# Order of the six projections of a tile, place of the norms behind them, and the means of the first norm in a fused attention and feed-forward kernel

## The chip, the cores and the metric

The kernel runs on one core of a Trainium2 chip. The metric is the time of one execution on the device, in microseconds (us); the time before is the median of three runs. The profile is that of one execution. Engines are called PE (TensorE, matmuls), PEld (its weight loads), DVE (VectorE), ACT (ScalarE), POOL (GpSimd) and SP (the engine that issues the DMAs).

## What is computed

The input x has 16 sequences of 256 positions with 128 channels. It goes through a first attention (windows of 64, 16 heads of 8 channels, a layer norm ahead of it and one on queries and keys), and then through a second block: a layer norm and six layers, each of a local attention and a gated feed-forward part. Cut to what matters here:

```python
x = x + first_attention(layernorm(x))
y = layernorm(x)
for i in range(6):
    # local attention: 16 heads of 64, windows of 32 that see the one before
    q, k, v = split(shift_tokens(y) @ Wqkv[i])        # 128 -> 3 x 1024
    q, k = l2norm(q) * q_scale[i], l2norm(k) * k_scale[i]
    q, k = rotary(q), rotary(k)
    y = softmax(mask(8 * q @ k.T)) @ v @ Wo[i] + y
    # feed-forward: layer norm, two products, gelu
    a, gate = split(layernorm(shift_tokens(y)) @ W1[i] + b1[i])
    y = (a * gelu(gate)) @ W2[i] + b2[i] + y
return x + y
```

## The kernel before

**Two stages.** The first attention works on 8 units of 4 tiles of 128 positions, its steps for several units merged into one order. Its `row_stats` (lines 315 to 328) makes mean and spread of each row: for the norm ahead of the attention (`pre == "a"`) ACT takes four copies with accumulation (line 321), for the one behind it DVE takes one sum (line 323) and POOL scales it (line 324). It takes about the first 250 us of the span.

The main stage, six layers, goes over 192 tiles of 128 positions (32 a layer) as a pipeline: in the turn of tile t, PE does the projections of tile t (`stage_p`), the scores of tile t-1 (`stage_s`), the exponentials of t-2 (`stage_e`), the weighted sums of t-3 (`stage_v`), the output product of t-5 (`stage_w`), and a part of the feed-forward of earlier tiles (`stage_f`, which serves four tiles at once and is spread over four turns).

**The order of the work.** Each stage is a generator; `merge_at` (line 248) steps them in the order of places between 0 and 1 in a turn. `stage_p` is stepped at 0, 1/6, ... 5/6 (`AT_P`), the exponentials at 0.09 and 0.095, the weighted sums at 0.1 and 0.45, the output product at 0.47, the scores at 0.72. The feed-forward goes by `AT_F = ((0.86,), (0.06, 0.74, 0.88), (0.03, 0.27, 0.8), (0.1, 0.35, 0.6))`, one tuple for each of four turns: its steps are the centring (0.86), the spread with a logarithm and an exponential (0.06 of the second turn), three gelus (0.74, 0.88, and 0.03 of the third turn), three products with the other half (0.27, 0.8, 0.1), the last matmul (0.35) and the end. PE's instructions keep exactly this recorded order, since `pin` (line 253) chains every matmul (`mul`, line 290) and transpose (`flip`, line 293) to the one before. The other engines' instructions are ordered by the framework's scheduler within their dependencies.

**Two extra orders on ACT.** Gelu and the pair logarithm and exponential are in different activation tables, and a load stands where the table changes. The program keeps them apart by hand: `tab` (line 274) records a logarithm or exponential behind the last gelu recorded; `gelu` (line 280) records the first gelu of a group behind all `tab` instructions recorded since the last first gelu, and the others only behind the gelu before. Behind the third gelu the program puts a load of the table that holds both logarithm and exponential (line 892).

```python
def tab(*args, **how):
    made = S.activation(*args, **how)
    if opened:
        behind(made, opened[-1])
    before.append(made.ins)
```

**A tile's projections.** `project` (line 626) makes three matmuls of 512 columns into one of two banks used in turn (kind "p"), with four of the waiting transposes (`turn`: the keys, queries and probabilities of earlier tiles) hung on them. The kernel before goes through keys, keys, queries, queries, values, values (`for s in (1, 0)`, line 648: s is 1 for keys, 0 for queries; two halves of 8 heads each). Behind a key or query projection, DVE multiplies with the rotary table (line 656), ACT squares into `sq` (line 664), POOL adds the two rotary halves (line 667); behind a value projection ACT copies into `vb` (line 677), one of three buffers used in turn.

`norm` (line 639) closes a pair of halves: DVE sums the squares (line 640), ACT takes logarithm and exponential through `tab` (lines 641 and 642, recorded at line 275), POOL bounds the result and multiplies both halves (lines 643 and 646). The list `late` delays it: the norm of the keys is recorded with the first query projection (third place), that of the queries with the first value projection (fifth place). After the sixth projection SP issues the DMAs that copy `vb` into shifted buffers (lines 688 to 694), read by `stage_v` three tiles later.

The banks of kind "t", "w", "f" and of the first half of `stage_v` are four in one ring (`SPLIT`, `USE`, `USE_V`): transposes, the output product, the feed-forward and the first half of the weighted sums take them one after the other.

Of the kernel before, what the change touches and what calls it, by code (L numbers as in the profile page):

```python
# [14 lines left out]
AF = mybir.ActivationFunctionType  # L15
ALU = mybir.AluOpType
AX = mybir.AxisListType
# [5 lines left out]
NV = 3  # L23
# [32 lines left out]
def kernel(  # L56
# [23 lines left out]
    V, S, G, T = nc.vector, nc.scalar, nc.gpsimd, nc.tensor  # L80
# [193 lines left out]
# [5 lines that stand above are left out]
# [11 lines left out]
    def mul(*args, **how):  # L290
        pin(T.matmul(*args, **how))  # L291
# [5 lines left out]
    def first_attention(p1, p2, p3, pqp, psp0, pop, pyp, ptp=None):  # L297
        ptp = ptp or pyp
        def rsqrt(dst, src, scale):
            if dst.shape[1] != 128:  # L300
                S.activation(dst, src, AF.Ln, bias=epst, scale=scale)
                S.activation(dst, dst, AF.Exp, scale=-0.5)
                return
            n = dst.shape[1]
            a = p3.tile([128, n], F32, name=f"rqa{n}")
            b = p3.tile([128, n], F32, name=f"rqb{n}")
            V.tensor_scalar(b, src, scale, EPS, ALU.mult, ALU.add)
            S.activation(a, b, AF.Ln)
            S.activation(a, a, AF.Exp, scale=-0.5)
            V.tensor_tensor(b, b, a, ALU.mult)  # L310
            V.tensor_tensor(b, b, a, ALU.mult)
            V.tensor_scalar(b, b, -0.5, 1.5, ALU.mult, ALU.add)
            V.tensor_tensor(dst, b, a, ALU.mult)

        def row_stats(xt, pre):
            mu = p3.tile([128, 4], F32, name=f"{pre}mu")
            rs = p3.tile([128, 4], F32, name=f"{pre}rs")
            sq = p3.tile([128, 128], F32, name="sq0")
            if pre == "a":
                for t in range(4):  # L320
                    S.activation(sq, xt[:, t], AF.Copy, scale=-1.0 / 128.0, accum_out=mu[:, t : t + 1])
            else:
                V.tensor_reduce(mu, xt, AX.X, ALU.add)
                G.tensor_scalar(mu, mu, -1.0 / 128.0, None, ALU.mult)
            for t in range(4):
                S.activation(sq, xt[:, t], AF.Square, bias=mu[:, t : t + 1], accum_out=rs[:, t : t + 1])
            rsqrt(rs, rs, 1.0 / 128.0)
            return mu, rs
# [39 lines left out]
        def stage_load(u):  # L368
            if u:
                load_x(u)  # L370
            e = U[u]
            _, e.rs = row_stats(e.xt, "a")
            e.rv = p1.tile([128, 4], F32, name="rv")
            G.tensor_scalar(e.rv, e.rs, VPRE, None, ALU.mult)
            yield
            e.xnt = p1.tile([128, 2, 4, 128], FR, name="xnt")
            pt = ptp.tile([128, 4, 128], F32, name="pt" if ptp is not pyp else "py")
            for t in range(4):
                T.transpose(pt[:, t], e.xt[:, t], ident)
            S.copy(e.xnt[:, 0], pt)  # L380
            V.tensor_tensor(e.xnt[:, 1], pt, e.xnt[:, 0].bitcast(F32), ALU.subtract)
            G.tensor_tensor(e.xt, e.xt, bpt.unsqueeze(1).to_broadcast([128, 4, 128]), ALU.add)
            yield
# [128 lines left out]
        def stage_norm(u):  # L512
            e = U[u]
            g, hb = divmod(u, 2)
            dma(r1d[g][:, 4 * hb : 4 * hb + 4], e.xt)
            mu, rs = row_stats(e.xt, "b")
            xn = p3.tile([128, 4, 128], F32, name="xn")
            V.tensor_tensor(mu, mu, rs, ALU.mult)
            for t in range(4):
                S.activation(xn[:, t], e.xt[:, t], AF.Identity, bias=mu[:, t : t + 1], scale=rs[:, t : t + 1])  # L520
            yield
            pt = ptp.tile([128, 4, 128], F32, name="pt" if ptp is not pyp else "py")
            for t in range(4):
                T.transpose(pt[:, t], xn[:, t], ident)
            pb = pt.rearrange("p (b j) t -> p b (j t)", j=2)
            S.copy(xg[g][0:64, 2 * hb : 2 * hb + 2, 0:256], pb[0:64])
            S.copy(xg[g][64:128, 2 * hb : 2 * hb + 2, 1:257], pb[64:128])
            yield
# [31 lines left out]
    def bank(kind):  # L560
        n = USE.get(kind, kind)
        return banks[n].tile([128, 512], F32, name=f"bank{n}")
# [14 lines left out]
    vbs = [keep.tile([128, 2, 8, 65], F32, name=f"vb{n}") for n in range(NV)]  # L577
# [27 lines left out]
    def turn(k):  # L605
        for f in turns[:k]:
            f()
        del turns[:k]
# [17 lines left out]
    def project(d, n):  # L626
        pp = bank("p")
        for q, (a, c) in enumerate(((0, 0), (0, 1), (1, 0))):
            mul(pp, d.xhl[:, a, d.j], wqs[d.i % 2][n][:, c], start=(q == 0), stop=(q == 2))
            turn(2 if q == 1 else 1)  # L630
        return pp

    def stage_p(t):
        d = tiles[t]
        tq = tqs[d.i]
        d.nat = {}
        late = []

        def norm(r, sq, mcs):
            V.tensor_reduce(r, sq, AX.X, ALU.add)  # L640
            tab(r, r, AF.Ln, bias=tiny)
            tab(r, r, AF.Exp, scale=-0.5)
            G.tensor_scalar(r, r, 1e12 / WPRE, None, ALU.min)
            for hb, mc in enumerate(mcs):
                rb = r[:, hb * 8 : hb * 8 + 8]
                G.tensor_tensor(mc, mc, rb.unsqueeze(2).to_broadcast([128, 8, 64]), ALU.mult)  # L646

        for s in (1, 0):
            r = front.tile([128, 16], F32, name="r", bufs=3)
            sq = front.tile([128, 16, 64], F32, name="sq", bufs=2)  # L650
            mcs = []
            for hb in range(2):
                pp = project(d, 2 * s + hb)
                p4 = pp.rearrange("p (h f d) -> p h f d", f=2, d=32)
                prod = front.tile([128, 8, 2, 2, 32], F32, name="mc", bufs=2)
                V.tensor_tensor(  # L656
                    prod,
                    p4.unsqueeze(3).to_broadcast([128, 8, 2, 2, 32]),
                    tq[:, s, d.j].unsqueeze(1).to_broadcast([128, 8, 2, 2, 32]),
                    ALU.mult,  # L660
                )
                mc = front.tile([128, 8, 64], F32, name="sum", bufs=NSUM)
                m2 = prod.rearrange("p h f g d -> p h f (g d)")
                S.activation(  # L664
                    sq[:, hb * 8 : hb * 8 + 8], pp.rearrange("p (h d) -> p h d", d=64), AF.Square
                )
                G.tensor_tensor(mc, m2[:, :, 0], m2[:, :, 1], ALU.add)  # L667
                mcs.append(mc)
                while late:
                    norm(*late.pop())  # L670
                yield
            late.append((r, sq, mcs))
            d.nat[s] = mcs
        d.vb = vb = vbs[t % NV]
        for hb in range(2):
            pp = project(d, 4 + hb)
            S.copy(
                vb[:, :, hb * 4 : hb * 4 + 4, 0:64],
                pp.rearrange("p (m a d) -> p a m d", a=2, d=64),
            )  # L680
            while late:
                norm(*late.pop())
            if hb == 0:
                yield
        d.v31 = work.tile([128, 8, 65], F32, name="v31", bufs=3)
        d.vw2 = work.tile([128, 8, 65], F32, name="vw2", bufs=3)
        d.vw0 = vw0[t % 4]
        dma(d.v31[64:128], vb[0:64, 1])
        dma(d.v31[0:64], vb[64:128, 0])
        for a in range(2):  # L690
            dma(d.vw2[64 * a : 64 * a + 64], vb[32:96, a])
            dma(d.vw0[64 * a : 64 * a + 32], vb[96:128, a])
            if d.j:
                dma(d.vw0[64 * a + 32 : 64 * a + 64], tiles[t - 1].vb[0:32, a])
        yield
# [216 lines left out]
    for t in range(total + 3 if LAYERS else 0):  # L912
# [8 lines left out]
        for lag, places, stage in (  # L921
            (0, AT_P, stage_p),
            (LAG_P, AT_E, stage_e),
            (LAG_V, AT_V, stage_v),
            (LAG_W, AT_W, stage_w),
            (LAG_S, AT_S, stage_s),
        ):
            if 0 <= t - lag < (total if t < total + 2 else 0):
                parts.append((places, stage(t - lag)))
# [102 lines left out]
```

## Time and profile before

| | |
|---|---|
| median of three runs | 3234.64 us (3232.51 to 3235.36) |
| the profiled execution | 3233.52 us |
| its span | 3231.7 us |
| busy share of the span: PE / DVE / POOL / ACT | 92% / 79% / 78% / 74% |
| main stage, first projection of tile 0 | at 249.8 us |
| table loads: line 281 / line 892 | 48 / 47, 1.283 us each |
| ACT in the first 32 us | busy 28.0 us |

Shares are averages over stages with different limits. A busy PE is one with a matmul in flight; its granted clock (1.00 is full speed) stands beside it in the tables by stretches. Where an engine was idle before an instruction, the profile names what released it; with several semaphores it names the one that came last, and where that was long done the cause was another.

### The profile page before, as it was taken

Reading aid. Unit: us, or ns where it says so; the run is one execution under the profiler, and the core shown is the slowest. Engines: PE = TensorE matmul, PEld = TensorE weight load, DVE = VectorE, ACT = ScalarE, POOL = GpSimd, SP = SyncE. Lnnn points to the kernel's source line nnn. Section 1 sums busy time; section 2 is a strip of 40 time slices with the busy share of each in tenths; the row PEclk is TensorE's granted clock in tenths of the full one; section 3 lists DMA queues with packets and bytes.
Section 4 is the critical chain, followed back from the end, with each engine's and each line's share of the span. In section 5 each row is a group of like instructions: output and inputs, shape, how many; then the busy total and the mean of one; then the engine's idle time right before and its main releaser. Section 6 shows DMA issues by size and latency. Waiting matters only on the chain. (4 is left out here: it accounts for less than half of the span.)

```text
span 3231.7 us, 152140 instructions
## 1 busy us (share of the span) xinstructions
PE 2969.9 (92%) x67106; PEld 2067.8 (64%) x67106; DVE 2559.5 (79%) x4306; ACT 2378.0 (74%) x4968; POOL 2536.6 (78%) x2594
## 2 busy tenths in 40 slices
PE   4778999999999999999999999999999999999997
PEld 3555666666666666666666666666666666666664
DVE  6887887887787887788787788887788888778774
ACT  7877777777777777777777777777777777777774
POOL 6768887788788778788788788788888778877872
PEclk6558999999999999999999999999999999999998
DMA  5773444444444443354444444443444444334433
GB/s 119 147 135 74 102 100 98 88 83 88 92 98 94 87 95 82 83 106 99 84 87 91 86 95 105 87 87 82 90 98 98 87 90 88 82 89 103 92 87 72
DMA packets 622935, 302.90 MB, mean 94 GB/s; under 512 B 533446, under 2 KB 545732, under 8 KB 622276
## 3 DMA queue, kind: packets, MB, share of 16 engines
q1 hardware_dynamic: 622276, 293.18, 42.6%
q8 instruction: 528, 8.65, 1.1%
q14 instruction: 131, 1.07, 0.1%
HBM read 22.45 MB, written 4.19 MB: 8 GB/s over the span
## 5 line engine op out<-in xcount | busy, mean ns | idle before, releaser
L291 PE MATMUL bank<-wqkv,xhl 128*128 128x512 f16 x3456 | 1229.9, 381 | 65.6 <-ACT sq L664 40.3
L656 DVE TENSOR_TENSOR mc<-bank,tq 128x1024 f32<-128x1024 f32 x768 | 929.0, 1221 | 185.8 <-PE bank L294 165.9
L667 POOL TENSOR_TENSOR sum<-mc 128x512 f32<-128x512 f32 x768 | 990.3, 1300 | 49.7 <-DVE mc L656 40.7
L646 POOL TENSOR_TENSOR sum<-sum,r 128x512 f32<-128x512 f32 x768 | 797.8, 1059 | 31.9
L294 PE MATMUL bank<-ident,sum 128*128 128x128 f32 x3072 | 711.2, 273 | 1.4 <-POOL sum L646 1.4
L806 POOL TENSOR_TENSOR ohl<-of,ohl 128x512 f16<-128x512 f32 x384 | 451.7, 1177 | 312.3 <-ACT ohl L805 312.1
L640 DVE TENSOR_REDUCE r<-sq 128x16 f32<-128x1024 f32 x384 | 465.2, 1211 | 168.3 <-ACT sq L664 168.2
L294 PEld LDWEIGHTS bank<-ident,sum 128*128 128x128 f32 x3072 | 432.9, 141 | 195.7 <-issue 83.4
L664 ACT ACTIVATE sq<-bank 128x512 f32<-128x512 f32 x768 | 466.6, 608 | 86.9 <-DVE mc L656 82.2
L291 PEld LDWEIGHTS <-xhl 128*128 128x128 f16 x3456 | 337.8, 98 | 177.9 <-issue 17.4
L275 ACT ACTIVATE r<-r,tiny 128x16 f32<-128x16 f32 x384 | 118.2, 308 | 398.3 <-DVE r L640 262.0
L291 PEld LDWEIGHTS bank<-vb,pt 64*32 64x32 f32 x6144 | 253.7, 105 | 164.9 <-issue 93.4
L294 PE MATMUL bank<-ident,p 128*128 128x128 f32 x1536 | 354.9, 273 | 0.7 <-issue 0.7
L805 ACT CAST ohl<-of 128x512 f16<-128x512 f32 x384 | 239.7, 624 | 150.2 <-DVE of L801 139.4
L291 PE MATMUL bank<-vb,pt 64*32 64x65 f32 x6144 | 340.8, 224 | 2.4 <-ACT pt L620 0.5
L291 PE MATMUL bank<-vw,pt 64*32 64x65 f32 x12288 | 336.7, 225 | 1.1 <-issue 1.1
L291 PE MATMUL bank<-v,pt 64*32 64x65 f32 x6144 | 315.6, 225 | 16.7 <-ACT gt L281 13.2
L291 PE MATMUL bank<-ot,wohl 128*128 128x128 f16 x4608 | 292.3, 220 | 3.2 <-DMA ot<-ohl 1.6
L801 DVE TENSOR_TENSOR of<-bank,rc 128x256 f32<-128x256 f32 x768 | 292.0, 416 | 3.2
L291 PE MATMUL bank<-kt,qt 64*32 64x64 f32 (+1 forms) x24576 | 285.1, 222 | 1.5 <-issue 1.5
L291 PEld LDWEIGHTS bank<-kt,qt 64*32 64x32 f32 x24576 | 256.6, 105 | 45.2 <-issue 45.0
L291 PEld LDWEIGHTS <-wohl 128*128 128x128 f16 x4608 | 259.3, 98 | 22.4 <-issue 3.9
(154 smaller groups left out, 5130.5 us busy)
## 6 DMA issues: line engine op xcount, KB each, us to landing
v<-vb SPq DMA_DIRECT2D x384, 130.0 KB
vw<-vb SPq DMA_DIRECT2D x384, 130.0 KB
vw<-vb SPq DMA_DIRECT2D x576, 65.0 KB
wraw<-in_L_ffn_Wqkv_dram SPq DMA_DIRECT2D x36, 256.0 KB
wraw<-in_L_ffn_Wo_dram SPq DMA_DIRECT2D x12, 256.0 KB
ot<-ohl SPq DMA_TRANSPOSE x192
xt<-in_L_attn_x_dram SPq DMA_DIRECT2D x8, 256.0 KB
r1d<-xt SPq DMA_DIRECT2D x8, 256.0 KB
```

Source lines behind the costliest of these rows:

```text
L275: made = S.activation(*args, **how)
L291: pin(T.matmul(*args, **how))
L294: pin(T.transpose(*args))
L640: V.tensor_reduce(r, sq, AX.X, ALU.add)
L646: G.tensor_tensor(mc, mc, rb.unsqueeze(2).to_broadcast([128, 8, 64]), ALU.mult)
L656: V.tensor_tensor(prod, p4.unsqueeze(3).to_broadcast([128, 8, 2, 2, 32]), tq[:, s, d.j].unsqueeze(1).to_broadcast([128, 8, 2, 2, 32]), ALU ...
L664: S.activation(sq[:, hb * 8 : hb * 8 + 8], pp.rearrange("p (h d) -> p h d", d=64), AF.Square)
L667: G.tensor_tensor(mc, m2[:, :, 0], m2[:, :, 1], ALU.add)
L801: V.tensor_tensor(of[:, :, a], po[a][:, :, 0:64], rc.unsqueeze(2).to_broadcast([128, 4, 64]), ALU.mult)
L805: S.copy(ohl[:, 0, h], of)
L806: G.tensor_tensor(ohl[:, 1, h], of, ohl[:, 0, h], ALU.subtract)
```

## The change

It has two parts.

In `stage_p` the order becomes keys, keys, values, queries, queries, values: the loop over s now takes, behind the two halves of the keys (s = 1) and behind those of the queries (s = 0), one half of the values (`vh = 1 - s`). The norm of the pair follows directly behind that value projection's copy, without the list `late`. The keys' norm so stays at the third place; the queries' norm moves from the fifth to the sixth. There are six steps as before, and the DMAs stay behind the sixth.

In `row_stats` the means ahead of the first attention are taken as those behind it were: one DVE sum for a unit and a scaling on POOL, in place of four ACT copies with accumulation.

```diff
@@ row_stats
-            if pre == "a":
-                for t in range(4):
-                    S.activation(sq, xt[:, t], AF.Copy, scale=-1.0 / 128.0, accum_out=mu[:, t : t + 1])
-            else:
-                V.tensor_reduce(mu, xt, AX.X, ALU.add)
-                G.tensor_scalar(mu, mu, -1.0 / 128.0, None, ALU.mult)
+            V.tensor_reduce(mu, xt, AX.X, ALU.add)
+            G.tensor_scalar(mu, mu, -1.0 / 128.0, None, ALU.mult)
@@ stage_p
-        late = []
+        d.vb = vb = vbs[t % NV]
         for s in (1, 0):
...
                 G.tensor_tensor(mc, m2[:, :, 0], m2[:, :, 1], ALU.add)
                 mcs.append(mc)
-                while late:
-                    norm(*late.pop())
                 yield
-            late.append((r, sq, mcs))
             d.nat[s] = mcs
-        d.vb = vb = vbs[t % NV]
-        for hb in range(2):
-            pp = project(d, 4 + hb)
+            vh = 1 - s
+            pp = project(d, 4 + vh)
             S.copy(
-                vb[:, :, hb * 4 : hb * 4 + 4, 0:64],
+                vb[:, :, vh * 4 : vh * 4 + 4, 0:64],
                 pp.rearrange("p (m a d) -> p a m d", a=2, d=64),
             )
-            while late:
-                norm(*late.pop())
-            if hb == 0:
+            norm(r, sq, mcs)
+            if s:
                 yield
```

## The prediction

> **What bounds the kernel now.** I read the page's totals first, then the stretches of the span, then ScalarE's timeline in the stretch where TensorE waits most, then the groups of instructions.
>
> The page's first lines, and one row of the table by stretches (columns: length; busy us and instructions of PE, PEld, DVE, ACT, POOL; granted clock; DMA share; GB/s) for the main stage without its ends:
>
> ```profile
> span 3231.7 us, 152140 instructions
> PE 2969.9 (92%) x67106; PEld 2067.8 (64%) x67106; DVE 2559.5 (79%) x4306; ACT 2378.0 (74%) x4968; POOL 2536.6 (78%) x2594
> 375.00:3140.00 2765.00, 2611.85 (x60109) 1818.78 (x60108) 2218.43 (x3668) 2048.73 (x4163) 2229.33 (x2265) 1.00 0.42 91
> ```
>
> TensorE is busy 94% of the main stage, at full clock, in an order written out by hand; what stops it costs its full length. The other engines have a fifth to a quarter free on the average, but not everywhere. In the feed-forward part, which comes once in four tiles (61.2 us from one load of L281 to the next), ScalarE's timeline (start, length, line, operation, tiles; in brackets idle before and releaser) reads:
>
> ```profile
> 1046.96 0.61 ACT L664 ACTIVATE sq<-bank 128x512 f32<-128x512 f32 x1
> 1048.92 0.31 ACT L275 ACTIVATE r<-r,tiny 128x16 f32<-128x16 f32 x1 [1.34 <-DVE r L640]
> 1049.26 0.21 ACT L275 ACTIVATE r<-r 128x16 f32<-128x16 f32 x1
> 1049.49 1.28 ACT L281 ACT_TABLE_LOAD   x1
> 1050.78 0.69 ACT L281 ACTIVATE gt<-bank,b1t 128x512 f32<-128x512 f32 x1
> ...
> 1052.14 0.60 ACT L620 COPY pt<-bank 128x512 f32<-128x512 f32 x1
> 1052.62 0.71 ACT L281 ACTIVATE gt<-bank,b1t 128x512 f32<-128x512 f32 x1
> 1053.20 0.61 ACT L622 COPY kt<-bank 128x512 f32<-128x512 f32 x1
> 1053.66 0.73 ACT L281 ACTIVATE gt<-bank,b1t 128x512 f32<-128x512 f32 x1
> 1054.41 1.28 ACT L892 ACT_TABLE_LOAD   x1
> 1055.71 1.08 ACT L275 ACTIVATE p<-bank 128x512 f32<-128x512 f32 x2
> 1056.68 0.60 ACT L664 ACTIVATE sq<-bank 128x512 f32<-128x512 f32 x1
> ```
>
> From 1049.49 to 1057.28 there is no gap: the row for that stretch has ACT busy 7.75 of 7.79 us. TensorE's timeline ends there with
>
> ```profile
> 1055.25 0.81 PE L291 MATMUL bank<-xnhl,w1hl 128*128 128x512 f16 x3
> 1057.34 0.38 PE L291 MATMUL bank<-wqkv,xhl 128*128 128x512 f16 x1 [1.27 <-DVE gt L896]
> ```
>
> This is a tile's third projection. It needs the bank that the first projection filled, and the last reader of that bank is the square ending at 1057.28; the named VectorE instruction is not its cause. So ScalarE is the bound in this stretch, and whatever is added to its queue between the first gelu and that square is added to the run.
>
> **The change part by part.** *The order on ScalarE.* The exponentials and logarithms are held behind the last gelu recorded (`behind` in `tab`), and only the first gelu of a group is held behind the ones before it. Gelus are recorded at 0.74 and 0.88 of a tile and 0.03 of the next (`AT_F`). The norm of the queries was recorded at 4/6, ahead of the first gelu; now it is recorded at 5/6, between the first and the second. The instruction order of the changed kernel as built shows the outcome: table load, gelu, **table load, logarithm, table load, exponential**, value copy, x copy, p copy, **table load**, gelu, k copy, gelu, table load, two exponentials of the scores, square. Three more loads stand in the chain, in 46 of the 48 groups (233 loads besides the first one, against 95). Their price:
>
> ```profile
> L281 ACT ACT_TABLE_LOAD x48 | 61.6, 1283 | 3.3 <-PE bank L291 2.5
> L892 ACT ACT_TABLE_LOAD x47 | 60.3, 1283 | 0.8
> ```
>
> 1283 ns each, with 4.1 us of idle before all 95. The chain from load to square was 7.79 us. Added are 3 x 1.283 = 3.85, the logarithm and exponential, formerly ahead of it (1048.92 to 1049.49, 0.57), and about 0.3 where a load must let an instruction end that its successor overlapped (the gelu at 1052.62 starts 0.12 before the p copy ends; twice, and gaps of 0.02): 12.5 us.
>
> When does it start? No longer after the logarithm, which waited 1.34 us for the sum of squares, but after the square of the second query projection. VectorE's order in the changed kernel, from the end of the second key product (1040.98: a pair of products starts at 1039.77, 1.21 each): xnhl 0.86, two reciprocals 0.3, two products of the output 0.8, sum of the keys' squares 1.2, two additions to x 0.6, two query products 2.4, together about 6.1; then the square 0.6: 1047.7 in place of 1049.49. So the square ends at 1047.7 + 12.5 = 1060.2 and not 1057.28: **2.9 us a group**. Bounds: 2.0 if VectorE runs 0.9 earlier (the wait for the output products before the mask's matmul, 33.8 us in all, is in this tile and should go), 4.7 if the start doesn't move. 46 x 2.9 = 133 (92 to 216).
>
> *The clock.* TensorE, after the scores' correction matmul (ends 1052.76 now), has nothing until p copy and second gelu have freed two banks: 1047.7 + 7.86 + 0.7 = 1056.2 (7.86: load to second gelu start by the new order). That is an idle of 3.4 to 4.8 us, where it is about half a microsecond now. Rows of the table by stretches at the span's end show what that does (clock: the third figure from the end):
>
> ```profile
> 3170.55:3173.96 3.41, 1.40 (x64) 1.07 (x62) 0.69 (x2) 1.90 (x4) 1.15 (x1) 1.00 0.76 212
> 3173.96:3177.37 3.41, 2.93 (x32) 2.76 (x33) 0.97 (x4) 0.62 (x1) 0.76 (x1) 0.50 0.11 29
> 3177.37:3180.79 3.42, 3.42 (x145) 2.90 (x144) 1.18 (x3) 1.07 (x2) 0.40 (x1) 1.00 0.58 110
> 1054.28:1057.70 3.42, 2.15 (x13) 1.28 (x13) 2.85 (x6) 3.39 (x7) 0.00 (x0) 1.00 0.49 130
> ```
>
> After 3.41 us in which PE was busy 41%, the next 3.41 us run at half clock, then full again; at 63% (last row, today's gelu stretch) the clock stays. The new idle leaves some window well below 41%, so I expect half clock in each group until a dense window has passed. That one begins between 1055.6 and 1059.0, wherever the grid of 3.41 us falls, and ends between 1059.0 and 1062.4. The work then due (half an output, a projection, a w1 product: 0.85 + 1.25 + 0.81 = 2.9 us) becomes 5.8; it has 4.0 until the third projection may start. What is left over is 0.4 to 2.1, I take 1.2: 46 x 1.2 = 55 (0 to 97, or twice that with two slow windows).
>
> *Here the Trainium skill speaks, and the sum does without it.* "TensorE: Matmul & The Clock Gate", Part 1, has the clock fall after at least one idle window of 3.4 us, the windows running freely. A gap of 4.6 us would then hold a whole window in about a third of the groups, an estimate from that page: some 19 us instead of 55. The rows above disagree: 41% busy was enough. "ScalarE: Activation LUTs", What ACT_TABLE_LOAD costs, puts 2.66 us on a switch, 1.38 of it a drain; that would make it 46 x 3 x 1.38 = 190 us more. The timeline shows 0.02 us ahead of a load and 0.01 behind it, so I leave the drain out. The same page says that logarithm then exponential take one load, as one set holds both; the order as built has two.
>
> *The rest of the steps.* The first value half (3 matmuls, a copy) moves from fifth to third place, the query projections one place later; PE's amount of work and the four transposes hung on each projection stay. Its copy now stands ahead of the second half of the output of three tiles ago, which reads the other half of that buffer, behind the first, which reads the same half. The DMAs of v31, vw2 and vw0 stay behind the last value copy, which slips by up to 2 us; they are read three tiles (46 us) later. Two query products now stand back to back before the sum, the maxima and the next key product. Where the feed-forward doesn't interfere, in two of four tiles, that puts the first key product 0.2 to 0.25 later by my count: 46 x 0.2 = 9 (0 to 20). The norm of the queries on POOL ends 0.9 to 5.4 us before its transposes today; 0.5 later leaves cover.
>
> *The first norm.* 32 copies with accumulation (309 + 188 ns) leave ScalarE: 16 us; VectorE gets 8 sums of 0.67 (as L323 has them), POOL 8 multiplications of 0.226: 7. In the first 32 us ACT is busy 28.0, so some of it ends late; later VectorE is the fuller. Between -16 and +7 I take -5.
>
> **Sum**: 133 + 55 + 9 - 5 = 192 on the profiled execution, 3233.5 us (span 3231.7 and 1.8 around it); it lies 1.1 under the median of the runs, 3234.6. Forecast **3425 us**.
>
> **The rivals.**
> - *No clock loss*: half clock does not come, or its work fits the 4.0 us. 133 + 9 - 5 = 137: 3370; 3330 with the low bound. For it: the 4 us to spare. Against: the rows above.
> - *Worse*: the chain starts no earlier (216) and the clock stays low for two windows (97 to 194): 3545. For it: between 35 and 250 us the clock stays at half over dense windows. Against: the main stage recovered in one at 262.
> - *Not slower, even faster*: ScalarE's other idle (262 us of waits for the sum of squares) takes the loads, and the smoother VectorE removes the 33.8 us before the mask: 3200 to 3235. It decides if the square that frees the bank is not behind the loads; the order as built puts it there, with ACT 7.75 of 7.79 full.
> - *The change doesn't do on the chip what the order says* (no further loads): 3234 - 5 and at most the 33.8 less, about 3200 to 3230; counted with the last.
>
> **How the numbers follow.** Forecast with its neighbourhood (3375 to 3470) 55%, no clock loss 22%, worse 18%, not slower 5%. The range 3335 to 3535 leaves out the last, the edge of the first rival and half of "worse". About 0.2% is what a measurement of this kernel can tell from no change: faster 4%, same 1%, slower 95%.
>
> **What would show it.** 138 more table loads, 92 of them at the line of `tab`; the third projection waiting 2.5 us and more once in four tiles; clock below 1.00 in slices of the main stage; a period of four tiles of 65 to 66 us instead of 61. A period under 62 with those loads present would prove me wrong on the chain; a clock of 1.00 throughout, on the second term.

## The result, and the profile after

The changed kernel takes **3479.61 us** (median of 4 runs, 3479.16 to 3482.22), beside 3234.77 us (3232.51 to 3235.36, 4 runs) for the kernel before on the same chip: a ratio of 1.076, 95% interval 1.0741 to 1.0779. That is 245 us more, where 191 had been forecast. The first lines of the page of the changed kernel, and its row for the main stage (columns as before: length; busy us and instructions of PE, PEld, DVE, ACT, POOL; clock; DMA share; GB/s):

```profile
span 3477.4 us, 152304 instructions
PE 3046.8 (88%) x67106; PEld 2110.8 (61%) x67106; DVE 2556.6 (74%) x4314; ACT 2550.4 (73%) x5042; POOL 2534.2 (73%) x2602
375.00:3370.00 2995.00, 2687.68 (x60197) 1862.34 (x60199) 2219.01 (x3671) 2228.25 (x4298) 2223.95 (x2263) 0.96 0.41 84
```

PE issues the same 67106 matmuls, at a mean clock of 0.96 where it was 1.00, and is busy 90% of the stage where it was 94%. ACT is busy 2550 us of the span, where it was 2378; the groups of its table loads say with what (count; busy, mean ns; idle ahead):

```profile
L281 ACT ACT_TABLE_LOAD x94 | 120.6, 1283 | 4.0 <-PE bank L291 2.4
L275 ACT ACT_TABLE_LOAD x92 | 118.0, 1283 | 1.6
L882 ACT ACT_TABLE_LOAD x47 | 60.3, 1283 | 0.8
```

There are 138 more than before: 92 new ones at the line of `tab`, 46 more at that of `gelu`. ACT's timeline in the stretch that the prediction worked on:

```profile
1122.24 1.28 ACT L281 ACT_TABLE_LOAD   x1
...
1124.24 1.28 ACT L275 ACT_TABLE_LOAD   x1
1125.54 0.31 ACT L275 ACTIVATE r<-r,tiny 128x16 f32<-128x16 f32 x1
1125.86 1.28 ACT L275 ACT_TABLE_LOAD   x1
...
1128.66 1.28 ACT L281 ACT_TABLE_LOAD   x1
...
1131.72 1.28 ACT L882 ACT_TABLE_LOAD   x1
1133.01 1.08 ACT L275 ACTIVATE p<-bank 128x512 f32<-128x512 f32 x2
1133.98 0.60 ACT L659 ACTIVATE sq<-bank 128x512 f32<-128x512 f32 x1
```

From the first load to the end of the square that frees the bank it is 1134.58 - 1122.24 = 12.34 us, where 7.79 had been the length before. TensorE at the same time (first matmuls of a group; in brackets the idle ahead):

```profile
1128.69 0.38 PE L291 MATMUL bank<-vb,pt 64*32 64x65 f32 x2 [2.78 <-ACT pt L616]
1130.69 0.32 PE L291 MATMUL bank<-v,pt 64*32 64x65 f32 x1 [1.62 <-ACT gt L281]
1131.80 0.61 PE L291 MATMUL bank<-wqkv,xhl 128*128 128x512 f16 x1
...
1135.19 0.59 PE L291 MATMUL bank<-wqkv,xhl 128*128 128x512 f16 x1
```

Two idles, 2.78 and 1.62 us, and behind them projection matmuls of 0.61 us that took 0.38 at full clock. The last line is the third projection: it starts 0.61 us after the square has ended, and PE was not idle ahead of it but still in its work at half clock. The table by stretches, cut along the clock's windows, shows why (clock: the third figure from the end):

```profile
1125.36:1128.77 3.41, 0.63 (x4) 0.13 (x3) 0.69 (x1) 3.35 (x8) 1.23 (x2) 1.00 0.00 0
1128.77:1132.19 3.42, 1.80 (x65) 1.20 (x66) 0.30 (x3) 3.39 (x5) 2.92 (x4) 0.50 0.69 175
1132.19:1135.60 3.41, 3.41 (x11) 1.81 (x10) 1.99 (x4) 3.40 (x7) 0.43 (x1) 0.50 0.06 20
```

A window in which PE is busy 18%, then two at half clock. Such a drop comes in 45 of the 46 groups, of two windows in 32 and of one in 13; the window ahead of it was busy 9% to 41%, by the trace's matmuls and clock record. The prediction's picture stands, but for its one window at half clock.

**Where the 245.7 us of the span lie.** By the starts of first projections: the head up to tile 0 is 4.5 longer (254.3 for 249.8), tiles 0 to 7 are 6.3, tiles 8 to 187 are 229.8 (2991.2 for 2761.4), the rest is 5.1. In tiles 8 to 185 I took the mean distance from one tile to the next by the remainder of the tile's number by 4; the gelus fall in remainder 2. All kernels at once, with their times; the ratio is to the kernel before on the same chip (on the several chips used it took 3230.64 to 3236.41, so that a difference between two of these kernels is sure only to some 6 us):

| kernel | us | ratio (95%) | 0 | 1 | 2 | 3 | sum |
|---|---|---|---|---|---|---|---|
| before | 3234.77 | | 13.39 | 15.70 | 16.86 | 15.40 | 61.35 |
| after | 3479.61 | 1.076 (1.0741, 1.0779) | 14.42 | 15.61 | 20.85 | 15.60 | 66.48 |
| e1 gelu behind the norm | 3327.93 | 1.0285 (1.0268, 1.0302) | 14.45 | 15.59 | 17.57 | 15.53 | 63.14 |
| e2 first norm only | 3238.58 | 1.0023 (1.0014, 1.0032) | | | | | |
| e3 norm later only | 3394.39 | 1.0489 (1.0474, 1.0505) | 13.39 | 15.70 | 20.44 | 15.33 | 64.86 |
| e4 two loads for three | 3409.57 | 1.0535 (1.052, 1.0551) | 14.48 | 15.63 | 19.15 | 15.51 | 64.77 |
| e5 idle filled | 3437.66 | 1.0624 (1.0608, 1.064) | 14.45 | 15.60 | 19.33 | 16.23 | 65.61 |
| e6 before, norm behind gelus | 3179.86 | 0.984 (0.9826, 0.9853) | 13.37 | 15.70 | 15.60 | 15.51 | 60.18 |
| e7 e1, square first | 3295.18 | 1.0197 (1.0181, 1.0212) | 14.05 | 15.38 | 17.59 | 15.53 | 62.55 |
| e8 e1, keys' sum later | 3349.66 | 1.0369 (1.0355, 1.0383) | 14.56 | 15.21 | 17.61 | 16.34 | 63.72 |
| e9 e7, maxima first | 3227.6 | 0.9971 (0.9962, 0.9981) | 14.01 | 14.85 | 16.74 | 15.35 | 60.95 |
| e10 all repairs | 3209.57 | 0.9921 (0.9906, 0.9935) | 13.98 | 14.73 | 16.35 | 15.49 | 60.55 |
| e11 e6, place and maxima | 3223.3 | 0.9965 (0.9952, 0.9977) | 13.87 | 15.90 | 15.59 | 15.51 | 60.87 |
| e12 after, maxima first | 3494.52 | 1.0802 (1.0786, 1.0818) | 14.31 | 14.98 | 22.19 | 15.33 | 66.81 |

There are 46 groups of four. Remainder 2 lost 3.99 us a group, but remainder 0 lost 1.03, where there is no gelu and no load.

Inside remainder 2 the traces give the places of the load, of the square that frees the bank and of the third projection, from the start of the tile (means of 44 groups):

| kernel | load ahead of the first gelu | square ends | third projection starts | next tile starts |
|---|---|---|---|---|
| before | -0.12 | 7.68 | 7.73 | 16.86 |
| after | -1.32 | 11.03 | 11.52 | 20.85 |
| e1 | 1.86 | 8.38 | 8.43 | 17.57 |
| e3 | -2.01 | 10.34 | 10.96 | 20.44 |
| e5 | -1.31 | 10.07 | 10.12 | 19.33 |
| e6 | -2.01 | 5.01 | 5.06 | 15.60 |
| e12 | -1.29 | 11.05 | 11.10 | 22.19 |

### The profile page after: what moved, and what is told of

Its sections match the earlier page's. It is cut to its first block, busy times and chain, and to the rows that moved or that the text cites. A ratio compares the mean times of both kernels' runs of the same rounds, so it can differ in the third digit from the quotient of the medians.

```text
span 3477.4 us, 152304 instructions
## 1 busy us (share of the span) xinstructions
PE 3046.8 (88%) x67106; PEld 2110.8 (61%) x67106; DVE 2556.6 (74%) x4314; ACT 2550.4 (73%) x5042; POOL 2534.2 (73%) x2602
## 5 line engine op out<-in xcount | busy, mean ns | idle before, releaser
L291 PE MATMUL bank<-wqkv,xhl 128*128 128x512 f16 x3456 | 1274.5, 393 | 35.4 <-ACT sq L659 33.9
L294 PE MATMUL bank<-ident,sum 128*128 128x128 f32 x3072 | 738.1, 282 | 0.3 <-POOL sum L640 0.3
L294 PEld LDWEIGHTS bank<-ident,sum 128*128 128x128 f32 x3072 | 450.6, 147 | 154.4 <-issue 33.5
L291 PE MATMUL bank<-vb,pt 64*32 64x65 f32 x6144 | 355.2, 232 | 129.3 <-ACT pt L616 129.3
L291 PEld LDWEIGHTS bank<-vb,pt 64*32 64x32 f32 x6144 | 263.9, 109 | 308.9 <-ACT pt L616 152.5
L637 POOL TENSOR_SCALAR r<-r 128x16 f32<-128x16 f32 x384 | 96.3, 251 | 437.1 <-ACT r L275 437.1
L291 PE MATMUL bank<-v,pt 64*32 64x65 f32 x6144 | 327.4, 234 | 77.0 <-ACT gt L281 76.4
L790 DVE RECIPROCAL rc<-bank 128x4 f32<-128x4 f32 x768 | 95.2, 165 | 395.4 <-PE bank L291 389.1
L291 PE MATMUL bank<-vw,pt 64*32 64x65 f32 x12288 | 346.2, 234 | 5.5 <-issue 5.5
L291 PEld LDWEIGHTS bank<-v,pt 64*32 64x32 f32 x6144 | 239.3, 110 | 88.4 <-ACT gt L281 85.2
```

The costliest lines, as they stand in the source:

```text
L294: pin(T.transpose(*args))
L790: V.reciprocal(rc, po[a][:, :, 64])
```

## The experiments

The theory after the result: table loads between the gelus lengthen ACT's chain, and the idle that this makes for PE costs half clock besides; the rest of the change is small. The rival: the order of projections itself costs most.

**e1: no loads between the gelus.** The first gelu is recorded behind the norm of the queries, so that one load serves all three again.

```diff
-AT_F = ((0.86,), (0.06, 0.74, 0.88), (0.03, 0.27, 0.8), (0.1, 0.35, 0.6))
+AT_F = ((0.86,), (0.06, 0.84, 0.88), (0.03, 0.27, 0.8), (0.1, 0.35, 0.6))
```

> The changed kernel with the first gelu's step moved from 0.74 to 0.84 of a turn, so that the queries' norm (5/6) is recorded ahead of it again; table loads by the built order: 48 + 47 as in the kernel before, and the new order of projections and the new first norm stay. Theory (three more loads in ScalarE's chain and the clock loss behind them): the period of four tiles falls by about 4 us, 184 us in all; what stays is the tile behind the feed-forward group (+1.0 us a group, about 47) and some 5 to 10 of the start: 3240 to 3295. Rival (the two query products back to back on VectorE are the cost): 3440 to 3480.

Measured 3327.93: 152 us better than after, all in remainder 2 (20.85 to 17.57), but above the range that the theory gave. 92 us are left that no load explains: the order costs too. (The first gelu also stands later in e1 than in the kernel before; what that costs was not run by itself, but the next run gives nearly the same without it.)

**e3: the place of the norm alone**, in the kernel before.

```diff
-            while late:
+            while late and hb:
                 norm(*late.pop())
```

> The kernel before with one edit: the queries' norm is recorded with the sixth projection and not with the fifth; order of projections and first norm as before. Loads by the built order: 233, as in the changed kernel. Theory: the stretch with the gelus pays three loads and the clock, 3.5 to 4.7 us a group: 3395 to 3450. Rival (order of projections): 3230 to 3240, since that order is not touched.

Measured 3394.39, 158 more than before, a hair below the range; only remainder 2 moves (16.86 to 20.44). e1 and e3 give the loads and what hangs on them from two sides: 152 and 158. What is left between e3 and the changed kernel, 85 us, is order and first norm, beside the 92 of e1.

**e4: two loads in place of three between the gelus.** The load of the table that holds logarithm and exponential together is put by hand behind the first gelu as well, and the later gelus wait for the pair.

```diff
-            behind(made, opened[-1])
+            behind(made, opened[-1], *before)
...
-            if n == 2 and not (last and final):
+            if n != 1 and not (last and final):
```

> The changed kernel with the table that holds both logarithm and exponential loaded behind the first gelu, and the later gelus held behind the logarithm and exponential: 2 more loads a group than before and not 3. Theory: one load of 1.28 us less in each of 46 groups: 59 us less, and up to 15 more if the idle gap, shorter by as much, costs less clock: 3405 to 3425. Rival (order of projections): 3480, no change.

Measured 3409.57: 70 us less for 44 loads less (189 for 233), 1.6 us a load of 1.283. Half clock falls with them: ahead of the third projection it lasts 3.11 us in a gelu tile of e4 on the mean, 5.45 in the changed kernel. That the rest of the 1.6 is clock alone was not shown.

**e5: PE kept busy in the idle.** 18 matmuls that add zero stand ahead of the mask's matmul in one tile of four; the loads stay.

```diff
+        for n in range(FILL if t % 4 == 0 and t >= 8 else 0):
+            mul(
+                pss[n % 2],
+                identh,
+                none.unsqueeze(2).to_broadcast([128, 8, 64]),
+                start=False,
+                stop=False,
+                skip_group_check=True,
+            )
```

> The changed kernel with 18 matmuls of zeros (identity times zero, added to the scores' banks) ahead of the scores' correction in the turn with the gelus, about 3.9 us at full clock, to fill most of TensorE's idle of 4.8 us there; three loads a group stay. Theory: the clock stays at 1.00 in the main stage and the work behind the gap is not slowed: 0.8 to 1.4 us a group, 3415 to 3445. Rival (the half clock costs nothing, since the work fits ahead of the square): 3475 to 3490.

Measured 3437.66, 42 us less. The main stage of e5, without its ends:

```profile
375.00:3325.00 2950.00, 2789.09 (x60864) 1897.07 (x60863) 2207.70 (x3664) 2222.11 (x4288) 2222.09 (x2260) 1.00 0.41 86
```

The clock is 1.00 throughout, and remainder 2 is 1.52 shorter (70 us in 46 groups); remainder 3 gives 0.63 of it back. But this is not the clock alone. With the new matmuls the order on ACT changed too: in all groups the square now stands ahead of the scores' exponentials, which it followed before.

```profile
1190.46 1.28 ACT L894 ACT_TABLE_LOAD   x1
1191.76 0.60 ACT L662 ACTIVATE sq<-bank 128x512 f32<-128x512 f32 x1
1192.25 1.08 ACT L276 ACTIVATE p<-bank 128x512 f32<-128x512 f32 x2
```

By the table above the square ends 0.96 us earlier for that (10.07 for 11.03). The clock's own share is read from the changed kernel: its third projection starts 0.49 us after the square, 0.05 in e5, e1 and before, and from there to the next tile it takes 9.33 us, 9.14 in e1. That is 0.44 + 0.19 = 0.63 us a group, 29 us in 46 groups. The same reading of e3, beside the kernel before, gives 0.57 + 0.35 = 0.92, or 42 us. Both are estimates; no run has the full clock and nothing else changed.

**e2: the first norm alone**, in the kernel before (the `row_stats` part of the change's diff).

> The kernel before with the means of the first norm by one VectorE sum a unit; main stage as before. Theory: it is worth little, between 8 us less and 5 us more: 3228 to 3241. Rival (a large part of what the order of projections seems to cost, 92 us with the loads taken away, comes from the first norm): 3260 and more.

Measured 3238.58 beside 3230.64: 8 us more, interval 0.14% to 0.32%. Tile 0 starts at 254.5 in place of 249.8, as it does in the changed kernel.

By now the change adds up, the order by difference: 152 (loads and clock) + 8 (first norm) + 84 (order, the rest of e1's 92; 77 by e3). The next three ask what in the order costs, starting from e1.

**e7: the square ahead of the value copy on ACT.** DVE's sum waits for the square of the second half; the value copy, now two places earlier, could stand ahead of it.

```diff
-                S.activation(
+                squared = S.activation(
...
-            S.copy(
+            copied = S.copy(
...
+            behind(copied, squared.ins)
```

> The changed kernel with the first gelu at 0.84 (as in the run with 3328), and each value copy on ScalarE held behind the square of the projection before it. In the trace of the changed kernel VectorE waits up to 1.9 us for that square, which stands behind the value copy and a copy of transposed queries. Theory (that wait is most of what the order costs): the four-tile period falls from 63.1 by 0.6 to 1.5 us, 3255 to 3300. Rival (the two query products back to back, or the bank of the sixth projection): 3320 to 3330.

Measured 3295.18: 33 us less than e1. That is inside the range, but not "most of what the order costs".

**e8: the keys' sum one place later**, behind the products of the output on DVE.

```diff
+                while late:
+                    norm(*late.pop(), firsts=outs)
                 yield
...
-            norm(r, sq, mcs)
             if s:
+                late.append((r, sq, mcs))
                 yield
+            else:
+                norm(r, sq, mcs)
```

> The same changed kernel with the first gelu at 0.84, with the keys' norm recorded with the fourth projection and its sum held on VectorE behind the second half of the output products, so that VectorE has these to do while it waits for the square. Theory: 0.4 to 1.2 us a group less than 3328: 3270 to 3310. Rival (query products back to back, bank of the sixth projection): 3320 to 3330, or more, as the keys' norm is later.

Measured 3349.66, 22 us worse than e1: a miss. Remainder 1 fell from 15.59 to 15.21, but remainder 3 grew from 15.53 to 16.34, and PE's waits for the score maxima from 18.7 to 42.1 us (between 260 and 3200 us). A later keys' norm is no repair.

**e9: the score maxima ahead of the queries' sum.** On DVE the sum of the queries' squares stands ahead of the two maxima of the scores, and waits for ACT. In the changed kernel (DVE, then the PE matmul that reads the maxima):

```profile
1159.92 1.22 DVE L634 TENSOR_REDUCE r<-sq 128x16 f32<-128x1024 f32 x1 [0.67 <-ACT sq L659]
1161.06 1.28 DVE L738 TENSOR_REDUCE nm<-bank 128x8 f16<-128x512 f32 x2
...
1161.79 0.38 PE L291 MATMUL bank<-nm,identh 128*128 128x512 f16 x1 [0.61 <-DVE nm L738]
```

DVE waits 0.67 us for the square and then sums for 1.2, with maxima behind it for which PE waits. The edit, on top of e7:

```diff
-            V.tensor_reduce(r, sq, AX.X, ALU.add)
+            made = V.tensor_reduce(r, sq, AX.X, ALU.add)
+            if s == 0:
+                behind(made, *maxima)
...
-            V.tensor_reduce(nm, pss[a], AX.X, ALU.max, negate=True)
+            maxima[a:] = [V.tensor_reduce(nm, pss[a], AX.X, ALU.max, negate=True).ins]
```

> The kernel of the run with 3295 (changed kernel, first gelu at 0.84, value copies behind the squares), with the sum of the queries' squares held on VectorE behind the two maxima of the scores. In that kernel TensorE waits 0.3 us a group for the maxima at the head of the tile after the feed-forward group, since VectorE stands idle for the square with the maxima behind it. Theory (what is left of the order's cost is VectorE's queue at the end of a tile): 0.3 to 0.8 us a group, 3260 to 3285. Rival (the sum, later by 1.3 us, makes TensorE wait for the queries' norm on POOL instead): 3295 to 3320.

Measured 3227.6, 68 us less than e7 and below the range. The same place in e9:

```profile
1087.11 1.29 DVE L742 TENSOR_REDUCE nm<-bank 128x8 f16<-128x512 f32 x2
1088.31 1.21 DVE L635 TENSOR_REDUCE r<-sq 128x16 f32<-128x1024 f32 x1
```

No wait ahead of either. The maxima themselves were the smaller part of what PE waited for: between 260 and 3200 us its waits for them (15.1 us in e7) and for the copy of the probabilities on ACT (29.6) are gone in e9 but for 0.5, and that for the input of the spread fell from 45.6 to 19.8; against that 24.5 us for POOL are new. With 33 + 68 us removed, the order's 84 are more than paid back, and the kernel is 0.3% faster than the one before. So a part of the 101 may be gain that the order before would have had too; this edit alone was not run in it.

**e6: the other way out, in the kernel before.** If a logarithm ahead of the first gelu delays the gelus, it can go behind the third. Only logarithm, exponential and POOL's half of the norm move, in one tile of four; the sum stays.

```diff
             V.tensor_reduce(r, sq, AX.X, ALU.add)
+            if wait:
+                held.append((r, mcs))
+            else:
+                scale(r, mcs)
...
-                norm(*late.pop())
+                norm(*late.pop(), wait=t % 4 == 1 and 9 <= t < total - 3)
...
+        if held:
+            parts.append(((0.05,), release(t)))
```

The exponentials of the scores are held behind it as well.

> The kernel before, with the scaling half of the queries' norm (logarithm, exponential, POOL's multiplications) recorded behind the third gelu in the turns that have the first gelu, so that ScalarE's load for the gelu needn't wait for the sum of squares; two loads a group as before. Theory (ScalarE's chain from the load to the square sets the period of the group): the chain starts 1.9 us earlier and holds 0.6 more, so 0.8 to 1.4 us a group: 3170 to 3200. Rival (TensorE's own order is the bound there, or its transposes of the queries wait for POOL instead): 3225 to 3250.

Measured **3179.86**, 1.6% faster than before and the best here. ACT's timeline behind the third gelu of e6:

```profile
1102.86 1.28 ACT L909 ACT_TABLE_LOAD   x1
1104.15 0.31 ACT L275 ACTIVATE r<-r,tiny 128x16 f32<-128x16 f32 x1
1104.36 0.58 ACT L671 ACTIVATE sq<-bank 128x512 f32<-128x512 f32 x1
1104.84 0.20 ACT L275 ACTIVATE r<-r 128x16 f32<-128x16 f32 x1
```

The pair uses the load that the scores' exponentials need anyway, and the square that frees the bank passes the exponentials. So the edit does two things: by the table of places the load starts 1.89 us earlier than before, and the square comes 0.78 sooner behind it. Of these 2.67 us remainder 2 shows 1.26, for the other rival came in part: PE waits 1.19 us a group for POOL's half of the norm (54.9 us, the row shown under e11).

**e10: everything together.** The changed order with the edits of e6, e7 and e9, the first gelu at 0.74, and the first norm as before:

```diff
+            if s == 0 and t % 4 == 1 and 9 <= t < total - 3:
+                held.append((r, mcs))
+            else:
+                scale(r, mcs)
```

> The changed kernel's order of projections with everything repaired: scaling half of the queries' norm behind the third gelu, value copies behind the squares, maxima ahead of the queries' sum, means of the first norm as in the kernel before, first gelu at 0.74 again. Theory (the order itself has no gain to give: what it takes away before the mask's matmul comes back before the feed-forward's next matmul): no faster than 3180, the kernel before with only the norm behind the gelus; 3185 to 3230. Rival (the smoother order is worth the 34 us of waits before the mask once its side effects are gone): 3140 to 3165.

Measured 3209.57: 0.8% faster than before, 30 us slower than e6. The order of projections brought nothing in any form tried.

**e11: is the place of the norm free?** e6 with the queries' norm at the sixth projection and its sum behind the maxima.

```diff
-            while late:
-                norm(*late.pop(), wait=t % 4 == 1 and 9 <= t < total - 3)
+            while late and hb:
+                norm(*late.pop(), firsts=maxima, wait=t % 4 == 1 and 9 <= t < total - 3)
```

> The kernel of e6 (the order before; logarithm and exponential of the queries' norm behind the third gelu), with the change's place for that norm (sixth projection) and its sum held behind the two score maxima on VectorE. Theory (the place of the norm costs nothing by itself; what it cost was table loads, and in the changed order a sum that stood ahead of ready work): no further loads, period of four tiles at most 60.5, 3150 to 3185 us. Rival (the sum one place later leaves POOL too little time ahead of the transposes): 3190 us and more.

Measured 3223.3, 43 us above e6: the rival holds, the theory's range does not. The loads between the gelus did not come back (98 loads in all for 95). What PE waited for, first e6, then e11 (us in total, times, longest):

```profile
PE bank L295 <- POOL sum L653: 54.9, 46, 1.4
```

```profile
PE bank L295 <- POOL sum L655: 75.0, 63, 1.4
```

PE waits 20 us longer for POOL's products ahead of the transposes, and 12 us longer for the square (12.5 and 24.7). Since e3, with the norm at the same place and its sum not held, left remainders 0, 1 and 3 where they were, it is the hold on the sum that costs here, I think; that was not run by itself. So the edit that won 68 us in e9 is no gain here, where one query product, not two, stands ahead of the sum.

**e12: the maxima ahead of the sum in the changed kernel itself**, all loads kept: the diff of e9, without the edits of e1 and e7.

```diff
+            if s == 0:
+                behind(made, *maxima)
```

> The changed kernel with one edit: the sum of the queries' squares is held on VectorE behind the two score maxima; all 233 loads stay. Theory (part of the loss beside the loads is this sum's place in VectorE's queue, worth 68 us where the loads were gone, but here the wait for the loads stands in one tile of four whatever VectorE does): 3400 to 3430 us, the gain in the three tiles without gelus. Rival (the chain on ScalarE sets the time and VectorE's order is hidden behind it): 3470 to 3485 us.

Measured 3494.52, 15 us *worse* than after and above both ranges. In remainders 0, 1 and 3 the theory's gain is there (1.01 us a group, 46 us), but remainder 2 lost 1.34. The third projection of a gelu tile in e12:

```profile
1132.62 0.58 PE L291 MATMUL bank<-wqkv,xhl 128*128 128x512 f16 x1 [1.45 <-ACT sq L662]
1133.21 0.63 PE L291 MATMUL bank<-wqkv,xhl 128*128 128x512 f16 x1
```

It and what follows run at half clock; in the changed kernel half clock was nearly over when the third projection began. From the trace's clock record, half clock per gelu tile lasts 5.45 us ahead of the third projection's start and 0.37 behind it in the changed kernel, 2.59 and 4.47 in e12. PE had its earlier work done sooner, and fell idle directly ahead of work that was late. From the third projection to the weighted sums, from there to the output product and from there to the fourth projection it takes 2.22 + 1.11 + 1.89 us (means of 44 groups) in place of 1.36 + 0.79 + 1.35: 1.72 more, with PE at work all the time. The third projection itself starts 0.42 earlier in the tile, which leaves 1.30 of the 1.34.

## Why the prediction was right in sign and range, and where it was wrong

- **What bounds the stretch, and the chain.** Right. The five loads stand where the built order had them, and the chain is 12.34 us long (12.5 worked out). 1283 ns a load, no drain: right. The chain starts 1.2 us earlier in the tile than before, where 1.8 had been taken, and the square that frees the bank ends 3.35 later (11.03 for 7.68), where 2.9 had been taken (2.0 to 4.7). Of these, 0.7 are there without any load (e1, 8.38) and belong to the order; e3, which has the loads and the order before, ends 0.69 ahead of the changed kernel. The 2.65 of the loads are 122 us in 46 groups, where 133 had been taken.
- **The clock.** Right in mechanism, too dear in size: 1.2 us a group were taken, 55 us (0 to 97); the traces give about 0.63, or 29 (0.92 and 42 in e3). Half clock mostly lasted two windows, as the rival "worse" had it, but PE did most of that work before the square had ended. So the sign "third projection waiting 2.5 us and more" did not come: PE's idle, 4.40 us in the group shown (3.4 to 4.8 forecast), stands ahead of the weighted sums and behind their first two matmuls, and directly ahead of the third projection there is none. "TensorE: Matmul & The Clock Gate", Part 1, of the Trainium skill, has the clock fall after at least one idle window; here windows 9% to 41% busy were enough, in nearly every group.
- **Loads and clock together**: 188 forecast, 152 and 158 measured (e1, e3). Over-estimated by a fifth, most of it in the clock.
- **"Two query products now stand back to back ... 46 x 0.2 = 9 (0 to 20)".** This step failed: the order costs 77 to 84. I had priced the delay of the next key product and not what stands in line: a value copy ahead of the square (33, e7) and, above all, a sum that waits for that square ahead of maxima that PE needs (68, e9). The two together are more than the order costs, as said under e9. The prediction named "the sum, the maxima and the next key product" in a row and did not ask which of them someone waits for.
- **The first norm**: -5 forecast, 8 measured; +7 had been the upper end. ACT was relieved as said (23.81 us busy in the first 32, for 28.03), but tile 0 starts 4.5 us later. In the five traces with the first norm as before tile 0 starts at 249.8 to 253.8 us, in the nine with the new one at 254.3 to 257.4, so a part of the 4.5 can be the execution; the 8 us are medians of 11 and 15 runs. What is late there I did not trace.
- **The wait ahead of the mask** (33.8 us) went, as said. Another took its place: PE's wait for the spread's input (L856, the squares of the centred rows) is 58.9 us, for 10.7 before (L866). These 48 us are as much as remainder 0 lost (1.03 us in 46 groups).
- **The rivals.** "No clock loss" falls with the windows at 0.50 and the third projection late behind the square, by 0.44 us a group. "Worse" came half: two windows at half clock, but a chain that did start earlier. "Not slower" falls with the period of 66.48 us with all its loads (65 to 66 had been given as the sign).

The forecast lay 54 us low because loads and clock were 30 to 36 too dear and the order and the first norm some 81 to 88 too cheap: errors of opposite sign, so that it was nearer than its parts, which is luck. Its near neighbourhood, 3375 to 3470, was missed by 10 us; the range held. What e12 adds: these parts are not independent. Measured without loads the maxima's place is worth 68 us; with the loads it is worth less than nothing, since clock lost behind the wait for the square costs more (1.72 us, e12) than clock lost ahead of it (0.44, changed kernel).

"ScalarE: Activation LUTs", Table sets: the hidden batching unit, of the Trainium skill, says that one set serves logarithm and exponential, so that the pair takes one load. The runs bear that out only where the load of that set was put by hand (e4, one load for the pair); where the placing was left to the program's build, the pair took two, 92 in all.

## What to carry to other kernels

Before a step moves in a kernel with hand-made orders, list what each in-order engine will have next to each other, and ask of every instruction that waits who waits behind it: the costly ones here were a logarithm between two gelus (three table loads) and a sum ahead of ready maxima. Move the small instruction that needs the other table to where that table is loaded anyway; that, with the scores' exponentials held behind it, made the old kernel 1.6% faster. And after an edit look at the order on the other engines as well: the matmuls of zeros in e5 let a square pass two exponentials, and the run was no longer one of the clock alone. And do not sum up what repairs are worth one by one: the same edit gave -68, +15 and, with a place, +43 us in three kernels.

## What the runs showed of the hardware that was not expected

- Where half clock falls decides its price. In the changed kernel 5.45 us of it ahead of the third projection put that off by 0.44 us behind the square, since PE had to wait for the square anyway; in e12, where 4.47 us of it fall behind the wait, work of 3.50 us took 5.22.
- 828 matmuls of zeros on the engine that sets the end (67934 for 67106) kept the clock at 1.00, and the kernel was 42 us faster; a part of that is the changed order on ACT.
